# First block's q by seven products, the gate's sums behind the exponentials, one copy per slot handed to VectorE in slots 12 to 15

## The chip, the cores and the metric

The kernel runs on one core of one Trainium2 chip. The metric is the device time of one execution in microseconds (us). The kernel before took 3244.99 us, the median of three executions (3246.35, 3242.94 and 3244.99). TensorE multiplies, VectorE and ScalarE read its results out of PSUM, GpSimd does a few tiny steps, and SyncE only issues DMAs. Every engine works through its own instructions in the order in which they are written.

## The reference

A sequence of 4 x 2048 tokens of width 512 passes through windowed attention and then through a feed-forward layer whose weights are blended per group of tokens. All is float32.

```
x = x + layernorm(attention(layernorm(x)))       # 16 heads of 32, windows of 128 tokens
x = x + layernorm(ffn(layernorm(x)))

attention:  q, k, v = x @ w_qkv
            each window of 128 queries sees its own and both neighbouring windows of keys
            softmax over up to 384 keys, then attn @ v
ffn:        h = relu(x @ gate_w1.T + gate_b1)
            g = mean over tokens of (h @ gate_w2.T + gate_b2)        # 8 numbers per batch
            mW1 = W1 + sum_e g[e] * TW1[e] ;  mW2 = W2 + sum_e g[e] * TW2[e]   # 2048 x 512
            out = gelu(x @ mW1.T + mb1) @ mW2.T + mb2
```

## The kernel before, in words

**Two stages.** The attention stage does windowed attention for all 64 windows, and along with it the gate and the first part of the blending. The feed-forward stage follows it on the same core and blends the rest while it multiplies.

**Blocks, windows, slots.** A block is 512 tokens (16 blocks, `K`), a window 128 tokens (64, `W_`). A window is done in four slots of four heads each, so there are 256 slots; slot `i` belongs to window `i // 4` and group `g = i % 4`. The main loop issues for slot `i`, in this order: the scores of slot `i + 1` (`scores`, L599, and their negated row maxima on VectorE, L608); the transposes of the probabilities of slot `i` for each of its two or three key windows `j` (`turn`: TensorE L636, then a copy from PSUM to `prT`, L638); the lists `mid`; the exponentials of slot `i + 1` on ScalarE (`exponentials`, L621); the dense products of a later block (`dense`); the list `rest`; the blending; the reads of the dense products; and, in every second slot, the products with v (`values`, L654). Scores and exponentials are in float32 in a pair of PSUM tiles (`ps_s`, two tiles), both of which belong to one slot: the next slot's scores cannot be written before the four exponentials have read them.

**Projections by seven products.** A 512-wide projection of a block is done as a two-by-two block product with seven instead of eight half-size products (`products`, `product`, `produced`; in the loop `paired`, `pair_read`). It needs sums and differences of the weights' quarters (`left_factors`, four VectorE operations) and of the token block's quarters (`right_factors`, two operations in each of two parts), and several products are accumulated in one PSUM bank, which is read between them. For block 0 this is done for k and v only; its q is done by sixteen whole matmuls (`project`, L403), ahead of them. Block 0 is projected before the loop starts; there the four tiles of block 1 are normalized and transposed too (`place_tile`).

**The gate.** For blocks 0 to 13 the gate's first layer is done by seven products too, in the four slots `s0` to `s0 + 3`, with `s0 = 4 * (4 * (K + 3) - 5)` (28, 44, 60, 76, ...) for the earlier blocks. Its result stands in four quarters; each is put through ScalarE's relu, with the sum over tokens taken along (`gate_quarter_sum`, two ScalarE operations per quarter, L175). One quarter is summed straight from PSUM at the end of slot `s0 + 3`. The three others are summed from SBUF at the start of slots `s0 + 3`, `s0 + 4` and `s0 + 5`, ahead of the transposes' copies (list `early_reads`). The last block of a batch is followed by `means`, `experts`, `first_biases` and `second_biases` (`gate_end`), in slots `s0 + 5` to `s0 + 7`.

**The blending.** A generator (`mixer`) yields one step at a time: eight multiply-adds on VectorE over 128 x 1024 (L144), each on a 512 KB block that SyncE fetched three steps ahead, then one step of sums, and again. From slot 84 on, the list `MIXED` says how many steps each slot takes, by the slot's number modulo 16 (20 steps in 16 slots). The feed-forward stage takes fixed numbers of steps and stops when there are none left.

Of the kernel before, what the change touches and what calls it, by code (L numbers as in the profile page):

```python
# [9 lines left out]
F32 = mybir.dt.float32  # L10
# [6 lines left out]
P = 128  # L17
# [4 lines left out]
KC = D // P  # L22
TB = 512
WB = TB // W
# [6 lines left out]
QSCALE = float(E) ** -0.5  # L31
# [3 lines left out]
def sandwich(ctx: ExitStack, tc: tile.TileContext, x, w_qkv, gw1, gb1, gw2, gb2, w1, b1, w2, b2, tw1, tb1, tw2, tb2, out):  # L35
    nc = tc.nc
# [14 lines left out]
    Q = D // 2  # L51
# [280 lines left out]
    with ExitStack() as actx:  # L332
# [3 lines left out]
        ps_t = actx.enter_context(tc.tile_pool(name="ps_t", bufs=3, space=PSUM))  # L336
# [32 lines left out]
        def norm_stats(K, t):  # L369
            xs_of[K, t] = stats(x_of[K, t], f"a{K}_{t}")  # L370

        def norm_tile(K, t):
            xn = xn_of[K, t] = x_of.pop((K, t))
            normalize(xn, xn, xs_of.pop((K, t)))
# [13 lines left out]
        def projection(K, i):  # L388
            if i == 0 and K % 2 == 0:
                return wp.tile([P, KC, TB], F32, tag="q0", name=f"q_{K}")  # L390
            return qkvp.tile([P, KC, TB], F32, tag="qkv"[i], bufs=2 if i else 1, name=f"{'qkv'[i]}_{K}")

        def project(K, i, m, pm, kcs=range(KC)):

            if m == 0 and kcs[0] == 0:
                (q_of, k_of, v_of)[i][K] = projection(K, i)
            xnT = xnT_of[K]
            for kc in kcs:
                if i < 2:
                    l, r = wqkv[i][:, kc, ts(m, P)], xnT[:, kc, :]  # L400
                else:
                    l, r = xnT[:, kc, ts(m, P)], wqkv[2][:, kc, :]
                nc.tensor.matmul(pm, lhsT=l, rhs=r, start=(kc == 0), stop=(kc == KC - 1))  # L403

        def projected(K, i, m, pm):
            if i == 0:
                nc.scalar.mul(q_of[K][:, m, :], pm, QSCALE)
            elif i == 1:
                nc.vector.tensor_copy(k_of[K][:, m, :], pm)
            else:  # L410
                nc.scalar.copy(v_of[K][:, m, :], pm)

# [28 lines left out]
        lefts, rights, bank = {}, {}, {}  # L444
# [75 lines left out]
        def product(K, i, u, half, key=0):  # L520
            l, r, begins, _, _ = products[u]
            if begins and half == 0 and key:
                sc = ps_s.tile([P, 2, TB], F32, tag="sc", name=f"pm_{K}_{i}_{u}")
                bank[key] = sc[:, 0, :].rearrange("p (a b) -> p a b", a=2)
            elif begins and half == 0:
                bank[0] = ps_m.tile([P, 2, Q], F32, tag="pm", name=f"pm_{K}_{i}_{u}")
            if u < 2 and half == 0:
                rights.setdefault((K, False), {"11": xnT_of[K][:, :2, :Q], "21": xnT_of[K][:, 2:, :Q]})
            left, right = lefts[i][l], rights[K, False][r]
            for kc in range(2):  # L530
                a, b = (left, right) if i < 2 else (right, left)
                nc.tensor.matmul(  # L532
                    bank[key][:, half, :],
                    lhsT=a[:, kc, ts(half, P)],
                    rhs=b[:, kc, :],
                    start=(begins and half == kc == 0),
                    stop=True,
                    skip_group_check=True,
                )
# [90 lines left out]
        def turn(i, j):  # L630

            W_, g = divmod(i, KC)
            st = win[W_]
            pt = ps_t.tile([P, 4, W], F32, tag="pt", name=f"ptp_{i}_{j}")
            for r in range(4):
                nc.tensor.transpose(pt[:, r, :], st["pr"][g * 4 + r][:, ts(j, W)], ident)  # L636
            prT = work.tile([P, 4, W], F32, tag="prT", bufs=6, name=f"prT_{i}_{j}")
            nc.scalar.copy(prT, pt)  # L638
            st["prT"][g, j] = prT

        def values(i, n):
# [31 lines left out]
        first = {i: [] for i in slots}  # L673
        mid = {i: [] for i in slots}
        late = {i: [] for i in slots}
        early_reads = {i: [] for i in slots}
        for K in range(1, NBK):
            s0 = 4 * (4 * K - 5)
            if K > 1:
# [61 lines left out]
        for K, s0 in gate_at.items():  # L741
            first[s0 - 2].append(lambda K=K: load_gate(K))
            if K < 14:
                for part in range(2):
                    rest[s0 + part].append(lambda K=K, part=part: right_factors(K, part, 3))
                for g in range(KC):
                    dense[s0 + g] = (
                        lambda half, K=K, g=g: [
                            paired(K, 3, u, h)
                            for u in ((others[g], chain[g]) if others[g] is not None and half == 0 else (chain[g],))  # L750
                            for h in ((0, 1) if u not in chain else (half,))
                        ],
                        lambda K=K, g=g: gate_read(K, g, 0),
                        lambda K=K, g=g: gate_read(K, g, 1),
                    )

                for j, (row, col) in ((3, (0, 1)), (4, (1, 1)), (5, (0, 0))):
                    early_reads[s0 + j].append(
                        lambda K=K, row=row, col=col: gate_quarter_sum(K, row, col, quarter[row, col], quarter[row, col])
                    )  # L760
                if K % NBLK == NBLK - 1:
                    b = K // NBLK
                    means, experts, first_biases, second_biases = gate_end(b, hsum_of[b], spare_bank, spare)
                    rest[s0 + KC + 1].append(means)

                    mid[s0 + KC + 2].append(experts)
                    mid[s0 + KC + 3].append(second_biases)
                    rest[s0 + KC + 3].append(first_biases)
                continue
            for oc in range(KC):  # L770
                dense[s0 + oc] = (
                    lambda half, K=K, oc=oc: gate_tile(K, oc, half),
                    lambda K=K, oc=oc: gate_sum(bank[0], K, oc, hsum_of[K // NBLK], spare),
                )
# [102 lines left out]
        for t in range(WB):  # L877
            x_of[1, t] = load_tile(1, t, "x", 4)
        load_rest()

        sums = [
            lambda: left_factors(1),
            lambda: right_factors(0, 0),
            lambda: left_factors(2),
            lambda: right_factors(0, 1),
        ]
        for m in range(KC):
            pm = ps_t.tile([P, KC, P], F32, tag="pt", name=f"pm0_{m}").rearrange("p k t -> p (k t)")
            project(0, 0, m, pm)
            projected(0, 0, m, pm)  # L890
            sums[m]()
        for u in range(7):
            for i in (1, 2):
                for half in range(2):
                    product(0, i, u, half, i)
                produced(0, i, u, i)
            if u < WB:
                norm_stats(1, u)
            if 1 <= u <= WB:
                norm_tile(1, u - 1)  # L900
            if 2 <= u <= WB + 1:
                place_tile(1, u - 2, nc.vector.tensor_copy)
            if u == 2:
                left_factors(0)
        scores(0)
        exponentials(0, range(4))


        MIXED = (1, 0, 1, 1, 2, 1, 1, 2, 2, 1, 1, 1, 2, 1, 1, 2)
        for i in range(NS):  # L910
            W_, g = divmod(i, KC)
            nk = span_of(W_)[1]
            for f in first[i]:
                f()
            if i + 1 < NS:
                scores(i + 1)
            more = i + 1 < NS
            for f in early_reads[i]:
                f()
            for j in range(nk):  # L920
                turn(i, j)
            for f in mid[i]:
                f()
            if more:
                exponentials(i + 1, range(4))
            for f in aux[i]:
                f()
            if dense[i]:
                dense[i][0](0)
                dense[i][0](1)  # L930
            for f in rest[i]:
                f()
            if dense[i] and len(dense[i]) > 2:
                dense[i][2]()
            if i >= 84:
                for _ in range(MIXED[i % 16]):
                    next(blend)
            if dense[i]:
                dense[i][1]()
            if i >= PAIRS:  # L940
                for n in (i - 1, i) if i == PAIRS else (i,):
                    values(n, 0)
            elif i % 2 == 0:
                if i:
                    values(i - 1, 0)
                values(i, 1)
            for f in late[i]:
                f()
# [407 lines left out]
```

## Time and profile before

| what | value |
|---|---|
| median of three executions | 3244.99 us |
| profiled execution, its time / its span | 3242.52 us / 3240.1 us |
| TensorE busy | 3217.5 us (99% of the span) |
| TensorE weight loads busy | 2686.7 us (83%), beside the matmuls |
| VectorE busy | 2146.4 us (66%) |
| ScalarE busy | 1565.3 us (48%) |
| GpSimd busy | 665.9 us (21%) |
| mean granted TensorE clock | 0.999 |

"Busy" is the time in which an instruction of the engine was running. A busy TensorE can still be stretched: its matmuls' ends are modelled, so a matmul that waits shows in the distance between two starts before it shows as idle time. In a timeline row the columns are the start in us from the span's start, the length, the engine, the line, the operation, what it writes and reads, the shape, how many instructions were merged into the row, and, in brackets, the engine's idle time before it and what ended it. A float32 matmul shows as two instructions.

### The profile page before, as it was taken

Reading aid. Unit: us, or ns where it says so; the run is one execution under the profiler, and the core shown is the slowest. Engines: PE = TensorE matmul, PEld = TensorE weight load, DVE = VectorE, ACT = ScalarE, POOL = GpSimd, SP = SyncE. Lnnn points to the kernel's source line nnn. Section 1 sums busy time; section 2 is a strip of 40 time slices with the busy share of each in tenths; the row PEclk is TensorE's granted clock in tenths of the full one; section 3 lists DMA queues with packets and bytes.
Section 4 is the critical chain, followed back from the end, with each engine's and each line's share of the span. In section 5 each row is a group of like instructions: output and inputs, shape, how many; then the busy total and the mean of one; then the engine's idle time right before and its main releaser. Section 6 shows DMA issues by size and latency. Waiting matters only on the chain.

```text
span 3240.1 us, 59233 instructions
## 1 busy us (share of the span) xinstructions
PE 3217.5 (99%) x23166; PEld 2686.7 (83%) x23166; DVE 2146.4 (66%) x2989; ACT 1565.3 (48%) x4291; POOL 665.9 (21%) x843
## 2 busy tenths in 40 slices
PE   9999999999999999999999999999999999999999
PEld 7787878888787887878768888888888888888888
DVE  5666666888888888888865665667657776412212
ACT  3767777777777777777761222112222111222121
POOL 1111111111111111110012332323332323321222
PEclk9999999999999999999999999999999999999999
DMA  2111112455555445554577889998889998822332
GB/s 86 50 53 58 42 53 79 145 165 171 191 180 177 155 160 199 189 175 148 200 264 276 317 311 347 351 335 327 317 323 361 340 335 328 305 104 91 130 111 98
DMA packets 316120, 652.00 MB, mean 201 GB/s; under 512 B 22969, under 2 KB 89657, under 8 KB 295490
## 3 DMA queue, kind: packets, MB, share of 16 engines
q1 hardware_dynamic: 315842, 648.22, 57.2%
q8 instruction: 183, 3.00, 0.4%
q14 instruction: 95, 0.78, 0.1%
HBM read 538.03 MB, written 110.10 MB: 200 GB/s over the span
## 4 chain that ended last, share of the span: by engine, by line
PE 94%; DVE 2%; ACT 2%; DMA 1%; issue 0%; POOL 0%; SPq 0%; POOLq 0%; ACTq 0%; DVEq 0%
PE pm L473 22%; PE px L971 13%; PE ptp L636 10%; PE px L1069 10%; PE pz L1069 7%; PE pz L971 7%; PE sc L599 6%; PE po L654 5%; PE py L971 3%; PE py L1069 3%; PE py2b L1069 3%; DMA exps<-in_tw 1%; PE ptx L287 1%; PE pto L258 1%; PE pt_a L382 1%; PE pm L532 1%
## 5 line engine op out<-in xcount | busy, mean ns | idle before, releaser
L144 DVE SCALAR_TENSOR_TENSOR acc<-exps,g,acc 128x1024 f32<-128x1024 f32 x512 | 703.6, 1374 | 77.9 <-DMA exps<-in_tw 72.5
L608 DVE TENSOR_REDUCE nm<-sc 128x2 f32<-128x768 f32 (+1 forms) x512 | 449.9, 919 | 229.6 <-PE sc L599 224.4
L621 ACT ACTIVATE pr<-sc,nm 128x384 f32<-128x384 f32 (+1 forms) x1024 | 574.0, 595 | 9.1 <-DVE nm L608 8.9
L638 ACT COPY prT<-ptp 128x512 f32<-128x512 f32 x736 | 384.8, 595 | 262.1 <-PE ptp L636 261.2
L1008 ACT COPY py<-px 128x512 f32<-128x512 f32 x63 | 36.0, 571 | 783.8 <-PE px L971 783.6
L636 PEld LDWEIGHTS ptp<-ident,pr 128*128 128x128 f32 x2944 | 317.2, 141 | 102.0 <-issue 89.6
L636 PE MATMUL ptp<-ident,pr 128*128 128x128 f32 x2944 | 378.0, 278 | 0.0
L971 PE MATMUL px<-tT,w 128*128 128x256 f32 x1512 | 349.7, 379 | 0.6 <-DVE cpv L1031 0.6
L971 PEld LDWEIGHTS px<-tT,w 128*128 128x128 f32 x1512 | 287.1, 190 | 40.2 <-DVE cpv L1031 1.2
L599 PE MATMUL sc<-k,q 32*128 32x384 f32 (+2 forms) x2816 | 243.6, 422 | 5.7 <-ACT pr L621 5.5
L621 ACT ACTIVATION_READ_ACCUMULATOR pr<-sc,nm 128x1 f32 x1024 | 238.2, 233 | 0.0
L1069 PE MATMUL px<-w2s,u 128*128 128x256 f32 x1024 | 228.9, 379 | 0.7 <-ACT last L292 0.7
L1028 DVE TENSOR_TENSOR cpb<-pz,cpb 128x512 f32<-128x512 f32 x63 | 43.5, 690 | 280.0 <-PE pz L971 245.9
L1069 PEld LDWEIGHTS px<-w2s,u 128*128 128x128 f32 x1024 | 194.5, 190 | 27.3 <-ACT last L292 0.9
L91 POOL TENSOR_SCALAR ve_b<-mv_b 128x1 f32<-128x1 f32 x64 | 42.0, 657 | 819.2 <-DVE mv_b L89 819.2
L654 PEld LDWEIGHTS po<-prT,v 128*32 128x32 f32 x5888 | 152.2, 110 | 50.8 <-ACT pr L621 26.8
L654 PE MATMUL po<-prT,v 128*32 128x128 f32 x5888 | 189.7, 275 | 0.1
L599 PEld LDWEIGHTS sc<-k,q 32*128 32x128 f32 x2816 | 119.3, 183 | 76.8 <-issue 54.3
L1046 POOL TENSOR_TENSOR t<-u 128x512 f32<-128x512 f32 x64 | 84.9, 1326 | 463.2 <-ACT u L983 451.1
L473 PE MATMUL pm<-xnT,wqkv 128*128 128x256 f32 x720 | 173.4, 384 | 0.0
L1088 DVE TENSOR_TENSOR y<-px,mb 128x512 f32<-128x512 f32 x48 | 33.1, 690 | 192.8 <-PE px L1069 192.8
L473 PEld LDWEIGHTS pm<-xnT,wqkv 128*128 128x128 f32 x720 | 133.0, 191 | 19.1 <-ACT prT L638 2.3
(230 smaller groups left out, 5601.8 us busy)
## 6 DMA issues: line engine op xcount, KB each, us to landing
exps<-in_tw SPq DMA_DIRECT2D x512, 512.0 KB, 6.3
w2s<-m2d SPq DMA_DIRECT2D x112, 1024.0 KB, 7.2
acc<-in_w SPq DMA_DIRECT2D x64, 512.0 KB, 6.6
x<-in_x SPq DMA_DIRECT2D x64, 256.0 KB, 4.5
m1d<-acc SPq DMA_DIRECT2D x64, 256.0 KB, 6.7
m2d<-acc SPq DMA_DIRECT2D x64, 256.0 KB, 6.5
w<-m1d SPq DMA_DIRECT2D x16, 1024.0 KB, 7.8
fxT<-xTd SPq DMA_DIRECT2D x16, 1024.0 KB, 8.9
```

What stands on the lines that cost most here:

```text
L144: nc.vector.scalar_tensor_tensor(acc, ets.pop(n), g_all[b][:, e : e + 1], acc, ALU.mult, ALU.add)
L473: nc.tensor.matmul(bank[u not in chain][:, half, :], lhsT=a[:, kc, ts(half, P)], rhs=b[:, kc, :], start=(u not in (2, 3, 4) and half == kc ...
L599: nc.tensor.matmul(scs[r // 2][:, r % 2, col : col + nj * W], lhsT=q[rows, g, ts(W_ % WB, W)], rhs=k_of[kb][rows, g, j0 * W : (j0 + nj) * ...
L608: nc.vector.tensor_reduce(st["nm"][:, h : h + 2], scs[u][:, :, : nk * W], AX.X, ALU.max, negate=True)
L621: nc.scalar.activation(pr[:, : nk * W], scs[r // 2][:, r % 2, : nk * W], AF.Exp, bias=st["nm"][:, h : h + 1], accum_out=st["den"][:, h : h ...
L636: nc.tensor.transpose(pt[:, r, :], st["pr"][g * 4 + r][:, ts(j, W)], ident)
L638: nc.scalar.copy(prT, pt)
L654: nc.tensor.matmul(po[r * E : (r + 1) * E, n, :], lhsT=v_of[kb][:, jj, h * E : (h + 1) * E], rhs=prT[:, r, :], start=(j == 0), stop=(j == ...
L971: nc.tensor.matmul(bank[:, f, :], lhsT=factor[:, f, kc * P : (kc + 1) * P], rhs=right[:, kc, :], start=(start and f == 0 and kc == 0), sto ...
L1028: nc.vector.tensor_tensor(S["b"], Z, S["b"], ALU.add)
L1046: nc.gpsimd.tensor_tensor(t1s[c], b12, us[c][:, :, :Q], ALU.subtract)
L1069: nc.tensor.matmul(bank[:, t, :], lhsT=right(c - c % 2)[:, c % 2, ts(t, P)], rhs=w[:, c, :], start=(start and c == 0 and t == tiles[0]), s ...
```

## The change

Four things are changed.

1. The first block's q is done by the seven products as well. The three projections of block 0 now alternate: q, k, v of product 0, then of product 1, and so on. q and k use the two `ps_s` tiles for their banks, v uses the `ps_m` bank. The factors' sums come in another order (`right_factors(0, 0)` and `left_factors(0)` first), and block 1's tiles are normalized and placed at other points; the last two of them are copied out by ScalarE instead of VectorE. v's products 5 and 6 stand behind the first scores and exponentials.
2. The three quarter sums of the gate are issued at the end of slots `s0 + 2`, `s0 + 5` and `s0 + 6`, behind that slot's exponentials and dense reads, instead of at the start of `s0 + 3`, `s0 + 4` and `s0 + 5`. What follows at a batch's end (`means` to `second_biases`) is issued two slots later.
3. In slots 12 to 15 the copy of the third key window's transposes is done by VectorE instead of ScalarE.
4. The blending starts in slot 85 instead of 84, and slots with number 14 modulo 16 take two steps instead of one.

```diff
@@ product
-            left, right = lefts[i][l], rights[K, False][r]
+            if i in lefts:
+                left = lefts[i][l]
+            else:
+                j = int(l) - 11
+                left = wqkv[i][:, 2 * j : 2 * j + 2, :Q]
+            right = rights[K, False][r]
@@ turn
-            nc.scalar.copy(prT, pt)
+            if j == 2 and 12 <= i < 16:
+                nc.vector.tensor_copy(prT, pt)
+            else:
+                nc.scalar.copy(prT, pt)
@@ gate
-                for j, (row, col) in ((3, (0, 1)), (4, (1, 1)), (5, (0, 0))):
-                    early_reads[s0 + j].append(
+                for j, (row, col) in ((2, (0, 1)), (5, (1, 1)), (6, (0, 0))):
+                    behind[s0 + j].append(
                         lambda K=K, row=row, col=col: gate_quarter_sum(K, row, col, quarter[row, col], quarter[row, col])
                     )
-                    rest[s0 + KC + 1].append(means)
-                    mid[s0 + KC + 2].append(experts)
-                    mid[s0 + KC + 3].append(second_biases)
-                    rest[s0 + KC + 3].append(first_biases)
+                    rest[s0 + KC + 3].append(means)
+                    mid[s0 + KC + 4].append(experts)
+                    mid[s0 + KC + 5].append(second_biases)
+                    rest[s0 + KC + 5].append(first_biases)
@@ ahead of the loop
-        sums = [left_factors(1), right_factors(0, 0), left_factors(2), right_factors(0, 1)]   # as lambdas
-        for m in range(KC):
-            pm = ps_t.tile([P, KC, P], F32, tag="pt", name=f"pm0_{m}").rearrange("p k t -> p (k t)")
-            project(0, 0, m, pm)
-            projected(0, 0, m, pm)
-            sums[m]()
-        for u in range(7):
-            for i in (1, 2):
-                for half in range(2):
-                    product(0, i, u, half, i)
-                produced(0, i, u, i)
-            if u < WB:
-                norm_stats(1, u)
-            if 1 <= u <= WB:
-                norm_tile(1, u - 1)
-            if 2 <= u <= WB + 1:
-                place_tile(1, u - 2, nc.vector.tensor_copy)
-            if u == 2:
-                left_factors(0)
-        scores(0)
-        exponentials(0, range(4))
-        MIXED = (1, 0, 1, 1, 2, 1, 1, 2, 2, 1, 1, 1, 2, 1, 1, 2)
+        right_factors(0, 0)
+        left_factors(0)
+        between = {
+            (0, 2): [lambda: left_factors(1)],
+            (1, 1): [lambda: left_factors(2)],
+            (1, 2): [lambda: right_factors(0, 1)],
+            (2, 2): [lambda: norm_stats(1, 0), lambda: norm_stats(1, 1)],
+            (3, 1): [lambda: norm_tile(1, 0), lambda: norm_tile(1, 1)],
+            (3, 2): [lambda: norm_stats(1, 2), lambda: norm_stats(1, 3)],
+            (4, 1): [lambda: norm_tile(1, 2), lambda: norm_tile(1, 3)],
+            (4, 2): [lambda: place_tile(1, 0, nc.vector.tensor_copy)],
+            (5, 1): [lambda: place_tile(1, 1, nc.vector.tensor_copy)],
+            (6, 1): [lambda: scores(0), lambda: exponentials(0, range(4))],
+            (5, 2): [lambda: place_tile(1, 2, nc.scalar.copy)],
+            (6, 2): [lambda: place_tile(1, 3, nc.scalar.copy)],
+        }
+        turns_of = [(u, i) for u in range(5) for i in range(3)] + [(5, 0), (5, 1), (6, 0), (6, 1), (5, 2), (6, 2)]
+        for u, i in turns_of:
+            key = (1, 2, 0)[i]
+            for half in range(2):
+                product(0, i, u, half, key)
+            produced(0, i, u, key)
+            for f in between.get((u, i), ()):
+                f()
+        MIXED = (1, 0, 1, 1, 2, 1, 1, 2, 2, 1, 1, 1, 2, 1, 2, 2)
@@ loop over slots
-            for f in early_reads[i]:
-                f()
             for j in range(nk):
                 turn(i, j)
...
-            if i >= 84:
+            if i >= 85:
                 for _ in range(MIXED[i % 16]):
                     next(blend)
             if dense[i]:
                 dense[i][1]()
+            for f in behind[i]:
+                f()
```

`left_factors`, `right_factors`, `norm_stats`, `norm_tile`, `place_tile`, `scores` and `exponentials` are the same functions as before.

More of the change, by code (lines that the diff above doesn't have):

```diff
@@ L391, in projection @@
             return qkvp.tile([P, KC, TB], F32, tag="qkv"[i], bufs=2 if i else 1, name=f"{'qkv'[i]}_{K}")
[L393 to L411, printed above, removed]
         def left_factors(i):
@@ L675, in sandwich @@
         late = {i: [] for i in slots}
-        early_reads = {i: [] for i in slots}
+        behind = {i: [] for i in slots}
         for K in range(1, NBK):
@@ L879, in sandwich @@
         load_rest()
[L881 to L886, printed above, removed]
-        for m in range(KC):
-            pm = ps_t.tile([P, KC, P], F32, tag="pt", name=f"pm0_{m}").rearrange("p k t -> p (k t)")
-            project(0, 0, m, pm)
-            projected(0, 0, m, pm)
-            sums[m]()
-        for u in range(7):
-            for i in (1, 2):
-                for half in range(2):
-                    product(0, i, u, half, i)
-                produced(0, i, u, i)
-            if u < WB:
-                norm_stats(1, u)
-            if 1 <= u <= WB:
-                norm_tile(1, u - 1)
-            if 2 <= u <= WB + 1:
-                place_tile(1, u - 2, nc.vector.tensor_copy)
-            if u == 2:
-                left_factors(0)
-        scores(0)
-        exponentials(0, range(4))
-        MIXED = (1, 0, 1, 1, 2, 1, 1, 2, 2, 1, 1, 1, 2, 1, 1, 2)
+        right_factors(0, 0)
[23 more added lines that the diff above has]
+        MIXED = (1, 0, 1, 1, 2, 1, 1, 2, 2, 1, 1, 1, 2, 1, 2, 2)
         for i in range(NS):
```

## The prediction

> **What bounds the kernel now.** I read the page first: TensorE is busy for 3217.5 of 3240.1 us, so a change pays only through less matmul work or where TensorE stands still or runs slowly. TensorE's waits come next.
>
> ```profile
> PE 3217.5 (99%) x23166; PEld 2686.7 (83%) x23166; DVE 2146.4 (66%) x2989; ACT 1565.3 (48%) x4291; POOL 665.9 (21%) x843
> ```
>
> ```profile
> PE sc L599 <- ACT pr L621: 5.5, 11, 1.5
> PE ptx L287 <- ACT prT L638: 2.8, 10, 0.3
> PE pm L473 <- ACT prT L638: 1.8, 3, 0.6
> ```
>
> The columns are total, times, longest. All three name ScalarE as releaser. TensorE's timeline says where they lie: from the first block into slot 1, then in slots 13 to 16.
>
> ```profile
> 12.18 14.00 PE L403 MATMUL pm<-xnT,wqkv 128*128 128x512 f32 x32 [0.23 <-ACT xnT L384]
> 26.02 1.89 PE L532 MATMUL pm<-xnT,wqkv 128*128 128x256 f32 x8
> 27.75 1.89 PE L532 MATMUL pm<-wqkv,xnT 128*128 128x256 f32 x8
> ...
> 52.45 0.70 PE L599 MATMUL sc<-k,q 32*128 32x256 f32 x4
> 53.30 0.70 PE L599 MATMUL sc<-k,q 32*128 32x256 f32 x4 [0.15 <-DVE v L552]
> 55.00 0.70 PE L599 MATMUL sc<-k,q 32*128 32x256 f32 x4 [0.99 <-ACT pr L621]
> 55.91 0.70 PE L599 MATMUL sc<-k,q 32*128 32x256 f32 x4 [0.21 <-ACT pr L621]
> 56.54 1.51 PE L636 MATMUL ptp<-ident,pr 128*128 128x128 f32 x8
> 57.85 3.19 PE L473 MATMUL pm<-xnT,wqkv 128*128 128x256 f32 x8
> ...
> 62.19 1.09 PE L636 MATMUL ptp<-ident,pr 128*128 128x128 f32 x8
> ...
> 140.20 1.53 PE L636 MATMUL ptp<-ident,pr 128*128 128x128 f32 x12
> 141.57 0.63 PE L382 MATMUL pt_a<-ident,x 128*128 128x128 f32 x4
> ...
> 149.08 0.93 PE L599 MATMUL sc<-k,q 32*128 32x128 f32 x8 [1.46 <-ACT pr L621]
> ```
>
> Start to start, a product of four matmuls takes 1.73 us (26.02 to 27.75); the one at 57.85 took 3.13. The view by stretches says why: the granted clock was halved there. Its columns are length, the five engines' busy times with counts, clock, DMA.
>
> ```profile
> 57.06:60.48 3.42, 3.42 (x13) 2.86 (x12) 1.58 (x3) 2.97 (x10) 0.00 (x0) 0.50 0.00 0
> ```
>
> The gate's cost shows on ScalarE, here in slot 80:
>
> ```profile
> 560.86 1.53 PE L636 MATMUL ptp<-ident,pr 128*128 128x128 f32 x12
> 561.05 0.50 ACT L175 ACTIVATE g<-g,gb_sb 128x256 f32<-128x256 f32 x1
> 562.04 1.55 ACT L638 COPY prT<-ptp 128x512 f32<-128x512 f32 x3
> 562.67 0.66 PE L287 MATMUL ptx<-ident,x 128*128 128x128 f32 x4 [0.28 <-ACT prT L638]
> ```
>
> The copies normally start 0.70 us after the transposes (140.20, copy at 140.90), which would be 561.56; the early sum holds them until 562.04. TensorE then needs a buffer that the first copy frees: twelve transposes to the next group take 1.81 us, against 1.37 (140.20 to 141.57).
>
> **Part 1, the head.** Removed: sixteen whole matmuls, 13.84 us (12.18 to 26.02). Added: seven products, 7 x 1.73 = 12.11. That alone is 1.7 us less matmul work. For the rest I follow TensorE through the new order.
>
> The start stays at 12.18. The three weights landed at 10.15, 12.86 and 15.57 (the issue rows' landings) and are wanted at 12.18, 13.91 and 15.64: v's leaves 0.07, which I take as no wait. VectorE does six factor operations at 0.68 from 12.2 and four more, until 19.0; the first sums are wanted at 22.56 (six products later). left_factors(2) runs from 21.6 to 24.3, wanted at 26.0. Each bank is read while the two other projections multiply, 3.46 us, against reads of 0.6 to 0.7. So no wait until product 6: the 15 products of rounds 0 to 4 end at 38.13, a tile (0.43) and q's and k's product 5, another tile and their product 6 end at 45.9.
>
> The first half of scores(0) starts at 45.9; the second waits for VectorE's read of k's product 6, until 46.76, and ends at 47.4 (now the same: 53.30 after 52.45). v's product 5 runs to 49.13, a tile to 49.56, then 0.4 us of waiting for VectorE's read of that bank (0.69 plus latency), v's product 6 to 51.71, a tile to 52.14. scores(1) starts at 52.14, against 55.00. The exponentials of slot 0 are over by 49.4, so their release, 0.99 + 0.21 us now, is covered by v's two products. If these were shorter, the release at 49.4 would still precede 52.14 by 2.7 us.
>
> Next: transposes at 52.78, a product at full clock 53.7 to 55.4, values to 56.0. ScalarE copies a tile of block 1 until 52.85, the transposes until 54.5, then four exponentials at a pitch of 0.455 until 56.45. The second half of scores(2) waits for these, so slot 1's transposes start at 57.2, against 62.19: **5.0 us gained**, 2.9 up to scores(1) and 2.1 behind it, of which the half clock is 3.42 x 0.5 = 1.7. I take the clock at full because TensorE was busy for 2.21 of the 3.41 us ahead of the half-clock stretch, partly with scores of 0.70 each, and in the new order no 3.4 us stretch has under 2.5 us, mostly full products. Ends: 1.7 (matmul work alone, ScalarE setting the rest) and 6.2 (none of the three waits, 0.2 + 0.4 + 0.6).
>
> The Trainium skill, "TensorE: Matmul & The Clock Gate", Part 1, says that the gate halves the clock after an idle window of about 3.4 us and that the windows run freely. Its window length agrees with the 3.42 us here. By it the halving depends on where the window falls, so it need not have struck the other executions of the kernel before; then 1.7 us of my gain would not be there.
>
> **Part 2, slots 12 to 15.** They hold no dense products, and ScalarE's round sets them: fourth exponential over, second half of scores (0.86), transposes (0.70 to the first copy), three copies (0.52 pitch), four exponentials (2.24 in all). The round is 5.43 us (138.22 to 143.65 to 149.08). With two copies on ScalarE it is 0.5 shorter per slot, as long as the row maxima are there: in slot 14 the second ended at 141.3 and the exponentials began at 142.33, one copy earlier is 141.8. VectorE's copy, 0.69 us (the row of block 1's tiles), runs behind the maxima and is wanted only by values, about 1 us later; VectorE was busy for 4.55 of 5.43 us there, less in the other three. Slot 12 gains 0.5 on ScalarE, hidden by TensorE. Slot 13's xnT, xo and oT copies then finish at 134.7 instead of 135.2 and three copies become two, so its exponentials start 1.2 earlier and slot 14's scores follow 1.4 earlier; slots 14 and 15 add 0.6 each. Sum: **2.6 us**. Ends: 0 (maxima set the round instead) and 6.7, all that slots 13 to 16 exceed the time of the same matmuls elsewhere.
>
> **Part 3, the gate's sums.** Each costs ScalarE 1.0 us (two at a 0.5 pitch). Ten blocks lose 1.81 - 1.37 = 0.44, with the slot 6.46 long; three at a batch's start lose 0.9 (slot 65: 464.60 to 466.73 is 2.13 against 1.37, and its scores 0.17 more). 4.5 + 2.7 is 7.2; the block of slot 240 may give 0.3: **7.5 us**. In their new places they must fit ahead of the next copies. End of s0 + 2: ScalarE was free from 551.69 to 553.75, waiting for values. End of s0 + 5: free from 572.33 to 574.38, 2.0 us less the 0.5 at most by which slots move. End of s0 + 6: 2 us of waiting for values again. All are over 1.0. If that cover is gone, the copies behind are late by the excess, as now. The other end is 0: every wait comes back one slot on.
>
> At a batch's end, means to second_biases move two slots on, each over two slots that have transposes of their own. Same instructions, means still four us behind the sums; the DMA of the bias moves with them on SP, behind one more xo store. Between 0 and 0.5 x 3; I take 0, as slots 81 to 83 show no TensorE wait.
>
> **Part 4, the blending.** Eleven slots gain a multiply-add of 1.28 us, slot 84 loses two: nine more, exactly one round of eight and a sum, so the feed-forward stage does its work in the same phase, nine steps earlier. In slot 94 VectorE has the room:
>
> ```profile
> 658.43 0.68 DVE L730 TENSOR_TENSOR g<-pm,g 128x512 f32<-128x512 f32 x1
> 660.61 1.82 DVE L608 TENSOR_REDUCE nm<-sc 128x2 f32<-128x768 f32 x2 [1.49 <-PE sc L599]
> ```
>
> 1.28 fits in the 1.49 that it waits ahead of slot 95's maxima. SP issues one more 512 KB load in these slots; no multiply-add of the attention stage waits for one (the 72.5 us of such waits all lie in the feed-forward stage). Taken at 0, ends -1.9 (three feed-forward waits of 0.8, 0.7 and 0.6 gone, roughly) and +2.
>
> **Sum.** 5.0 + 2.6 + 7.5 = 15.1 us. The profiled execution took 3242.52 (2.4 outside its span) and would take 3227.4; the median is 2.5 higher, so 3244.99 - 15.1 = **3229.9 us**, 0.47% less.
>
> **The rivals.**
> - *The half clock was this execution's.* Gain 13.4, 3231.6. For it: the halving began on one particular stretch; against it: that stretch's stall is in the program's order.
> - *ScalarE sets the new head.* It has two tile copies more. Gain 1.7 + 2.6 + 7.5 = 11.8, 3233.2. Against it: it idles from 49.4 to 52.25 but for one copy.
> - *The moved sums wait again*, at s0 + 6 behind the sum of s0 + 5, where the margin is 0.5 to 1.0 us. Gain 7.6, 3237.4. That is also the case of a move that does nothing.
> - *Slower: the extra multiply-add waits for its block.* VectorE stands before L144 in eleven slots, and the maxima, exponentials and scores behind it stand too. A load lands 6.3 us after issue in the median, 11.7 at worst, and SP stood 340.8 us behind xo stores in this stage. It decides from 2.0 us per slot ((15.1 + 6.5) / 11); at 3 us it is 33 - 15 = 18 slower, 3263. Against it: the load goes out three steps ahead, and at today's 20 steps in 16 slots no wait occurs.
>
> **Chances and range.** Likeliest 0.60 (its own range 3226 to 3233), half clock 0.08, ScalarE 0.10, sums 0.10, slower 0.05, several small losses to between 3238 and 3250 0.07. This kernel's measurement can tell 0.2%, 6.5 us: faster is below 3238.5. The first four, less a part of the sums case, give 0.86; same 0.08; slower 0.06. The range is 3224 (the upper ends of parts 1 and 2 partly reached, 21 us) to 3239.
>
> **What would show it.** No half clock after 57; slot 1's transposes near 57; TensorE's wait for pr down from 5.5 to under 4; both rows that wait for prT gone; a round of 4.9 in slots 14 and 15; VectorE's wait of 1.49 down to 0.2. I would be wrong if L144 waits for its DMA before slot 255, or if prT waits reappear at s0 + 6.

## The result, and the profile after

The changed kernel took 3231.59 us, the median of six executions (3227.71 to 3233.09), against 3244.85 us for the kernel before on the same chip. The ratio is 0.996, with a 95% interval from 0.995 to 0.9971: 13.3 us faster, where 15.1 were forecast. The profiled execution took 3230.53 us, 12.0 less than the profiled one of before, so the sum below is made for 12.0.

The head of the page of the kernel after:

```profile
span 3228.7 us, 59302 instructions
...
PE 3211.8 (99%) x23190; PEld 2690.1 (83%) x23190; DVE 2142.8 (66%) x2995; ACT 1566.3 (49%) x4288; POOL 660.1 (20%) x843
```

TensorE is busy for 5.7 us less. Its waits in the kernel after (total, times, longest):

```profile
PE sc L584 <- ACT pr L606: 3.3, 9, 1.0
PE pt_a L382 <- DVE x L98: 1.4, 3, 0.7
PE idle L855 <- POOL ident masks.py:199: 1.3, 1, 1.3
PE pm L517 <- DMA wqkv<-in_w_qkv: 1.0, 2, 0.8
```

Both rows that waited for `prT` are gone, and the wait for `pr` is down from 5.5 to 3.3. The fourth row is new: TensorE waits for a weight. The timeline of the kernel after shows where, and what the other parts became:

```profile
11.29 1.89 PE L517 MATMUL pm<-xnT,wqkv 128*128 128x256 f32 x8
13.36 1.99 PE L517 MATMUL pm<-xnT,wqkv 128*128 128x256 f32 x8 [0.18 <-DMA wqkv<-in_w_qkv]
16.16 1.97 PE L517 MATMUL pm<-wqkv,xnT 128*128 128x256 f32 x8 [0.80 <-DMA wqkv<-in_w_qkv]
17.96 3.62 PE L517 MATMUL pm<-xnT,wqkv 128*128 128x256 f32 x16
...
46.55 0.70 PE L584 MATMUL sc<-k,q 32*128 32x256 f32 x4
47.41 0.70 PE L584 MATMUL sc<-k,q 32*128 32x256 f32 x4 [0.15 <-DVE k L537]
48.04 1.99 PE L517 MATMUL pm<-wsum,tx_False 128*128 128x256 f32 x8
...
50.82 1.99 PE L517 MATMUL pm<-wsum,xnT 128*128 128x256 f32 x8 [0.35 <-DVE v L537]
...
53.18 0.71 PE L584 MATMUL sc<-k,q 32*128 32x256 f32 x8
...
58.11 1.09 PE L621 MATMUL ptp<-ident,pr 128*128 128x128 f32 x8
...
135.14 1.53 PE L621 MATMUL ptp<-ident,pr 128*128 128x128 f32 x12
...
140.08 1.53 PE L621 MATMUL ptp<-ident,pr 128*128 128x128 f32 x12
...
554.54 1.53 PE L621 MATMUL ptp<-ident,pr 128*128 128x128 f32 x12
555.23 1.56 ACT L626 COPY prT<-ptp 128x512 f32<-128x512 f32 x3 [0.39 <-PE ptp L621]
555.90 0.62 PE L287 MATMUL ptx<-ident,x 128*128 128x128 f32 x4
```

Without waits the three products would start 1.73 us apart, at 11.29, 13.02 and 14.75; the third starts at 16.16, 1.41 late. Slot 1's transposes stand at 58.11 instead of 62.19. A round of slots 13 to 15 is 4.94 us (135.14 to 140.08) instead of 5.43. In slot 80 (the last three rows) the copies now start 0.69 behind the transposes, and the next group follows after 1.36, not 1.81.

And the half clock is still there, in the view by stretches (length, busy times of the five engines, clock, DMA):

```profile
57.06:60.48 3.42, 3.42 (x31) 2.82 (x24) 2.49 (x4) 2.68 (x9) 0.00 (x0) 1.00 0.00 0
144.62:148.04 3.42, 3.42 (x19) 2.77 (x16) 2.90 (x5) 1.17 (x2) 0.00 (x0) 0.50 0.01 2
141.20:144.62 3.42, 2.26 (x22) 1.58 (x22) 2.63 (x6) 3.38 (x11) 1.00 (x2) 1.00 0.04 13
```

It left the head, and struck slots 15 and 16 (the third row is the window ahead of it). The start of each slot's transposes, compared between the two profiled executions, gives the account:

| place | forecast, us | measured, us |
|---|---|---|
| first product, 12.18 to 11.30 | 0 | 0.89 |
| head, first product to slot 1 | 5.0 | 3.20 |
| slots 12 to 15 | 2.6 | 1.62 |
| half clock in slot 16 | 0 | -1.27 |
| gate's sums, slots 17 to 240 | 7.5 | 7.59 |
| slot 247 | 0 | -1.02 |
| feed-forward stage | 0 | 0.42 |
| outside the span (2.38 to 1.82) | 0 | 0.56 |
| sum | 15.1 | 12.0 |

The loss in slot 247 has this row on VectorE, which the kernel before does not have:

```profile
1620.67 0.55 DVE L98 TENSOR_SCALAR x<-x,mv_c,rs_c 128x512 f32<-128x512 f32 x1 [3.35 <-DMA x1d<-x]
```

The normalization overwrites `x1` in place, and waits until `x1` is stored.

### The profile page after: what moved, and what is told of

The parts are those of the page before. It is cut to its first block, busy times and chain, and to the rows that moved or that the text cites. A ratio compares the mean times of both kernels' runs of the same rounds, so it can differ in the third digit from the quotient of the medians.

```text
span 3228.7 us, 59302 instructions
## 1 busy us (share of the span) xinstructions
PE 3211.8 (99%) x23190; PEld 2690.1 (83%) x23190; DVE 2142.8 (66%) x2995; ACT 1566.3 (49%) x4288; POOL 660.1 (20%) x843
## 4 chain that ended last, share of the span: by engine, by line
PE 96%; DMA 2%; DVE 1%; ACT 1%; issue 0%; POOL 0%; SPq 0%; POOLq 0%; DVEq 0%; ACTq 0%
PE pm L453 23%; PE px L958 13%; PE ptp L621 11%; PE px L1056 10%; PE sc L584 7%; PE pz L958 7%; PE pz L1056 6%; PE po L642 5%; PE py L958 3%; PE py L1056 3%; PE py2b L1056 3%; DMA exps<-in_tw 1%; PE pm L517 1%; PE ptx L287 1%; PE pto L258 1%; PE pt_a L382 1%
## 5 line engine op out<-in xcount | busy, mean ns | idle before, releaser
L144 DVE SCALAR_TENSOR_TENSOR acc<-exps,g,acc 128x1024 f32<-128x1024 f32 x512 | 697.0, 1361 | 75.0 <-DMA exps<-in_tw 69.0
```

Of the source, the lines that this page charges most:

```text
L144: nc.vector.scalar_tensor_tensor(acc, ets.pop(n), g_all[b][:, e : e + 1], acc, ALU.mult, ALU.add)
```

## The experiments

**First, the parts apart.** Four kernels ran on one chip, where the kernel before took 3244.1 us. The first is the kernel before with the gate's sums moved, and nothing else:

```diff
-                for j, (row, col) in ((3, (0, 1)), (4, (1, 1)), (5, (0, 0))):
-                    early_reads[s0 + j].append(
+                for j, (row, col) in ((2, (0, 1)), (5, (1, 1)), (6, (0, 0))):
+                    behind[s0 + j].append(
...
-                    rest[s0 + KC + 1].append(means)
+                    rest[s0 + KC + 3].append(means)
```

> The kernel before with the gate's sums moved and nothing else. If the sums' place is what held the transposes' copies: ten slots shorten by 0.47 us each and three by 0.96 (the steps that the changed kernel shows at slots 32, 48, 65, 80 and so on), 7.6 us in all, and TensorE waits for no prT copy any more; about 3237 us. If part of that gain came from the slots' new position in time (the head's 4 us earlier, other DMA neighbours), fewer than 7 us. The half clock at 57 us stays.

It took 3235.96 us, ratio 0.9976 (0.9966 to 0.9985): 8.1 us. In its trace ten slots are 0.47 shorter and three pairs of slots at a batch's start 0.96, 7.6 in all, in the same slots as in the kernel after. The gate's part stands alone, at its forecast. The half clock at 57, which was expected to stay, is not in this profile; three others are.

The second is the kernel after with the gate's sums, the copies and the blending of before, so only the head is new:

```diff
-            if j == 2 and 12 <= i < 16:
-                nc.vector.tensor_copy(prT, pt)
-            else:
-                nc.scalar.copy(prT, pt)
+            nc.scalar.copy(prT, pt)
...
-                for j, (row, col) in ((2, (0, 1)), (5, (1, 1)), (6, (0, 0))):
-                    behind[s0 + j].append(
+                for j, (row, col) in ((3, (0, 1)), (4, (1, 1)), (5, (0, 0))):
+                    early_reads[s0 + j].append(
...
-            if i >= 85:
+            if i >= 84:
```

> The kernel before with the first block's new order and nothing else. Theory: slot 1's transposes come 3 to 4.1 us earlier than before (3.2 counted from the first product), v's weights are waited for again (0.8 to 1.1 us behind the second product), and no half clock follows at 57 us. Now the stretch in slots 12 to 16 is the kernel before's (rounds of 5.43 us): if low activity there is what halves the clock, it should be halved in slots 15 to 17 here too, or not at all if the windows fall otherwise; if it was the copy on VectorE that brought the half clock to 145 us, it stays at full.

It took 3238.17 us, ratio 0.9982 (0.9973 to 0.9992): 5.9 us. In its profile slot 1 starts 4.93 earlier, of which 1.3 is an earlier first product (10.86). Here a half clock began at 146.68 and took 1.65 back, and the feed-forward stage took 1.1 more than in the profile of before.

The third is the kernel before with VectorE's copy in slots 12 to 15:

```diff
-            nc.scalar.copy(prT, pt)
+            if j == 2 and 12 <= i < 16:
+                nc.vector.tensor_copy(prT, pt)
+            else:
+                nc.scalar.copy(prT, pt)
```

> The kernel before with the third copy of slots 12 to 15 on VectorE and nothing else. Theory: 0.49 us earlier per slot from slot 13 on, 1.6 to 2.1 us by slot 16's transposes. If the half clock depends on where its window falls, the head's half clock at 57 us is kept and slots 16 and 17 may run at full clock, 2 us gained at slot 17; if the copy itself brings it (TensorE less busy in each window of slots 14 to 16), it is halved at 145 to 151 us too and 0.3 us is left.

Its one execution took 3244.6 us, so the time tells nothing; its trace does. Slots 12 to 15 are 0.49 shorter each, 1.96 in all. Nothing is hidden in slot 12 and nothing is doubled in slot 13: every round is shorter by about one copy at ScalarE's pitch. And its clock was halved in four windows, in three places. Each row with a clock of 0.50 below is preceded by the window ahead of it:

```profile
51.59:55.00 3.41, 2.27 (x14) 0.90 (x12) 2.02 (x3) 1.76 (x8) 0.00 (x0) 1.00 0.00 0
55.00:61.83 6.83, 6.62 (x26) 4.77 (x28) 2.67 (x4) 3.21 (x13) 0.00 (x0) 0.50 0.01 2
147.16:150.58 3.42, 2.51 (x23) 1.78 (x24) 2.80 (x6) 2.29 (x10) 1.00 (x2) 1.00 0.03 5
150.58:153.99 3.41, 3.41 (x16) 3.14 (x15) 2.12 (x4) 3.05 (x8) 0.00 (x0) 0.50 0.00 0
1601.24:1604.65 3.41, 2.45 (x37) 1.31 (x38) 3.30 (x6) 3.20 (x11) 0.29 (x2) 1.00 0.87 317
1604.65:1608.06 3.41, 3.41 (x19) 2.76 (x16) 2.79 (x4) 0.98 (x2) 0.50 (x1) 0.50 0.62 187
```

Ahead of each halving TensorE was busy for 2.3 to 2.5 of 3.41 us.

The fourth is the kernel after with the old blending:

```diff
-            if i >= 85:
+            if i >= 84:
...
-        MIXED = (1, 0, 1, 1, 2, 1, 1, 2, 2, 1, 1, 1, 2, 1, 2, 2)
+        MIXED = (1, 0, 1, 1, 2, 1, 1, 2, 2, 1, 1, 1, 2, 1, 1, 2)
```

> The changed kernel with the old blending (from slot 84, one step in slots of number 14 modulo 16). If the nine steps that were brought forward are what puts the store of window 61's x1 among other transfers, the wait of VectorE for that store in slot 247 (3.35 us, which cost 1.0 us of TensorE) is gone; the feed-forward stage then is as long as before, 0.4 us more than in the changed kernel: 0.6 us less in sum. If that wait is chance or comes from the earlier arrival, it stays. Everything up to slot 240 within 0.1 us of the changed kernel, but for the clock's windows.

It took 3229.51 us, ratio 0.9955 (0.9938 to 0.9971). The wait in slot 247 is gone. By chance its first product, at 10.86, found v's weights landed at 14.19 and its products stand 1.73 apart: the head is the one that I forecast, 45.42 us from the first product to slot 1's transposes. It lost 1.09 to a half clock in slot 242, and its feed-forward stage took 1.4 more than in the profile of before, where the same length was expected.

**What the half clock follows.** Each of the six profiles so far shows it, in changing places. If a window with little matmul work is the cause, idle matmuls put into the thin slots must remove it from all. The next kernel is the fourth with such matmuls, whose result nothing reads; the computation is complete:

```diff
+        FILL = {13: 3, 14: 3, 15: 4, 240: 2, 241: 4}
...
+            if i in FILL:
+                filler = ps_m.tile([P, P], F32, tag="pm", name=f"fill_{i}")
+                for _ in range(FILL[i]):
+                    nc.tensor.matmul(filler, lhsT=ident, rhs=ident, start=True, stop=True)
```

> The changed kernel with the old blending, and with 3, 3, 4, 2 and 4 idle matmuls of 0.21 us behind slots 13, 14, 15, 240 and 241, where TensorE waits for exponentials. Theory: the clock is halved for 3.41 us after a window of 3.41 us in which the array did less than about 1.2 to 1.4 us of full-array work; with 0.6 to 0.9 us more in each window none stays under 1.5, so no half clock stands between 10 and 3200 us. It costs up to 0.3 us where the idle matmuls outlast the wait, and gains 1.0 to 1.7 us per half-clock stretch avoided, 2 us on average over executions: a median of 3227 to 3229 and a smaller spread. Rival: the halving goes by standing still, not by the array's work, or by something else; then half-clock stretches stand in these slots as before and the time is the same or 0.5 us worse.

It took 3228.87 us, ratio 0.9954 (0.9941 to 0.9966), and no stretch between the first products and the end is at half clock. Its median is no proof of a gain: the intervals of this ratio and the fourth's overlap. In this execution TensorE waited 0.8 us for v's weights again.

The next one also puts v's first product one place later, behind q's and k's:

```diff
-        turns_of = [(u, i) for u in range(5) for i in range(3)] + [(5, 0), (5, 1), (6, 0), (6, 1), (5, 2), (6, 2)]
+        turns_of = [(0, 0), (0, 1), (1, 0), (0, 2), (1, 1), (1, 2)] + [(u, i) for u in range(2, 5) for i in range(3)] + [(5, 0), (5, 1), (6, 0), (6, 1), (5, 2), (6, 2)]
```

> The same, and in the first block v's product 0 stands behind q's product 1, so that v's weights are wanted 1.73 us later. Theory: the weights land between 14.2 and 16.0 us, by execution, and v's product 0 wanted them 3.5 us after the first product: now 5.2 us after it, at 16 or later, so no wait for v's weights (k's may wait 0.2 to 0.3), and slot 1's transposes come 45.4 to 45.8 us after the first product in every execution; 0 to 1.1 us gained by execution, 0.5 in the median. Rival: VectorE's factors or the reads of the banks become late by the new order; then waits for VectorE appear at the first block's products.

It took 3227.36 us, ratio 0.9951 (0.9938 to 0.9963). Its timeline has no wait for weights; 24 matmuls run through:

```profile
11.42 5.35 PE L517 MATMUL pm<-xnT,wqkv 128*128 128x256 f32 x24
16.61 1.89 PE L517 MATMUL pm<-wqkv,xnT 128*128 128x256 f32 x8
```

The later versions with this order never wait for v's weights either, but two of their three profiles wait 0.38 and 0.25 for k's. Their heads take 45.99 and 45.85 us from the first product to slot 1's transposes, against 45.34 without any wait.

The same idle matmuls in the kernel before, with four more behind its first exponentials (both kernels already have some ahead of their first products; "with idle matmuls" means those added here):

```diff
         exponentials(0, range(4))
+        keep_busy(4)
...
+        FILL = {13: 3, 14: 3, 15: 4, 240: 2, 241: 4}
```

> The kernel before with the same idle matmuls and four more behind the first exponentials. Theory: half-clock stretches are gone from the head too, where three executions of the old order showed none, one and two of them (0, 1.4 and 2.8 us): about 1.4 us in the median there and 2 in the later slots, 3240 to 3242 us against 3244, and less spread. That would be the part of the changed kernel's gain that needed no other order of the work. Rival: no difference, if the halving doesn't go by the array's work.

It took 3240.72 us against 3242.67, ratio 0.9993 (0.9984 to 1.0003). No stretch is at half clock here either. Its head takes 48.66 us from the first product to slot 1's transposes, against 50.01 in the profile of before: the half clock there cost 1.35 us.

The stretches of half clock in all thirteen profiles, between the first products and the last ones:

| kernel | starts, us (3.41 us each) |
|---|---|
| before | 57.06 |
| after | 144.62 |
| gate only | 138.69, 148.93, 1596.18 |
| head only | 146.68 |
| copy only | 55.00 (two windows), 150.58, 1604.65 |
| after, old blending | 1589.42 |
| blending only | 149.13 |
| the six with idle matmuls | none |

Is it the time in which TensorE is busy, or the work that it does? Two windows at the same place, each with the window behind it, answer it: the first pair is from the kernel before, the second from the kernel before with the new blending alone (the next experiment), which is the same program up to slot 84.

```profile
145.81:149.22 3.41, 1.95 (x18) 1.68 (x19) 2.14 (x4) 2.89 (x8) 1.00 (x2) 1.00 0.00 0
149.22:152.63 3.41, 3.22 (x30) 2.44 (x31) 2.40 (x3) 2.28 (x7) 0.00 (x0) 1.00 0.02 5
145.72:149.13 3.41, 1.96 (x18) 1.23 (x19) 1.16 (x3) 2.80 (x10) 0.80 (x2) 1.00 0.02 5
149.13:152.54 3.41, 3.41 (x17) 3.41 (x17) 2.66 (x4) 2.02 (x4) 0.00 (x0) 0.50 0.00 0
```

TensorE was busy for 1.95 and 1.96 us of the first and the third row, and only the window behind the third was halved. Busy time alone does not decide it. What differs is which matmuls stood there. In the first window they are nearly all transposes, which use the array's 128 rows and 128 columns; in the third most are scores, which use 32 of the rows (`128*128` and `32*128` in the timeline rows). Counted as under "What is open" below, an estimate, the first held 1.6 us of whole-array work and the third 0.9.

**The blending.** The kernel before with the new blending alone ran beside the last three:

```diff
-            if i >= 84:
+            if i >= 85:
...
-        MIXED = (1, 0, 1, 1, 2, 1, 1, 2, 2, 1, 1, 1, 2, 1, 1, 2)
+        MIXED = (1, 0, 1, 1, 2, 1, 1, 2, 2, 1, 1, 1, 2, 1, 2, 2)
```

> The kernel before with the new blending alone. Theory: the nine steps brought forward cost nothing up to slot 240 and 1.0 us in slot 247 (VectorE waits over 3 us for the store of x1), give 0.4 us in the feed-forward stage: 0 to 1.5 us slower than before, not to be told from it. If slot 247 shows no wait, that wait was chance in the changed kernel's execution. If slots of number 15 modulo 16 lose time, VectorE has no room for the second step.

It took 3244.8 us, ratio 1.0007 (0.9998 to 1.0016). Its slot 247 waits too, for 5.2 us, and ends 2.9 us late, with nothing gained in the feed-forward stage (-0.07). To find the mechanism three more ran together, with idle matmuls so that no half clock blurs them. One is the version with v later, with the new blending:

> The version with idle matmuls and v's second product later, but with the blending of the kernel after (from slot 85, two steps in the slots with number 14 modulo 16). Theory (the phase of the round): in slots 239 to 253 the new blending is eight steps ahead, not nine, so the group of the blended matrix's stores and the reload of the next blocks is issued around slots 244 and 245 instead of 241, and the 256 KB store of x1 (slot 245) lands behind it some 7 us after its issue instead of 3.4; the normalization that overwrites x1 waits 3 to 5 us for it on VectorE and slot 247 ends 1.0 to 2.9 us late. No half-clock stretch. 1 to 3 us slower than the same kernel with the old blending in this call. Rival (the blending costs nothing, and the two slot-247 waits seen were single executions): same time within 0.7 us, no such wait.

It took 3229.87 us (3228.41 to 3230.57), ratio 0.9957 (0.9942 to 0.9971), with this on SyncE and VectorE:

```profile
1601.89 0.49 SPq L125 DMA_DIRECT2D m1d<-acc  x1
1602.48 0.40 SPq L126 DMA_DIRECT2D m1d<-sums  x1
1602.98 0.43 SPq L127 DMA_DIRECT2D m1d<-sums  x1
1603.46 1.16 SPq L128 DMA_DIRECT2D m1d<-acc  x1
1604.72 1.16 SPq L319 DMA_DIRECT2D w<-m1d  x2
...
1610.79 0.34 SPq L278 DMA_DIRECT2D x1d<-x  x1
...
1618.88 0.55 DVE L98 TENSOR_SCALAR x<-x,mv_c,rs_c 128x512 f32<-128x512 f32 x1 [4.27 <-DMA x1d<-x]
```

The next takes one step more in slot 237 and one less in slot 254:

```diff
-                for _ in range(MIXED[i % 16]):
+                for _ in range(MIXED[i % 16] + (i == 237) - (i == 254)):
```

> As the run before, with one more step of blending in slot 237 and one less in slot 254, so that slots 238 to 253 are nine steps ahead, a whole round. Theory (the phase): the group is issued around slot 241 again, the store of x1 lands within 3.5 us, no wait for it in slot 247; the time is that of the old blending within 0.7 us, or up to 0.5 us less. Rival (any blending that is ahead loads more in slot 245 and holds the store up): the wait in slot 247 stays at 3 to 5 us, and 1 to 3 us are lost as in the run before.

It took 3227.44 us (3226.49 to 3227.8), ratio 0.9949 (0.9936 to 0.9962). The four stores are issued 12 us earlier, and the wait is gone:

```profile
1589.56 0.49 SPq L125 DMA_DIRECT2D m1d<-acc  x1
1590.10 0.43 SPq L126 DMA_DIRECT2D m1d<-sums  x1
1590.57 0.48 SPq L127 DMA_DIRECT2D m1d<-sums  x1
1591.10 1.43 SPq L128 DMA_DIRECT2D m1d<-acc  x1
...
1602.09 0.94 SPq L319 DMA_DIRECT2D w<-m1d  x2
...
1610.95 0.34 SPq L278 DMA_DIRECT2D x1d<-x  x1
...
1614.69 0.54 DVE L98 TENSOR_SCALAR x<-x,mv_c,rs_c 128x512 f32<-128x512 f32 x1
```

The last is the version with v later and the old blending again.

> The version with idle matmuls, v's second product later and the old blending once more, as the partner of the two runs before on the same chip. Both theories: 3226 to 3229 us if the kernel before takes 3243, no wait for the store of x1 in slot 247, no half-clock stretch in the main loop.

It took 3227.1 us (3226.78 to 3227.47), ratio 0.9948 (0.9935 to 0.9961). The executions of the new blending lie wholly above those of the two others: the phase of the round, and not the earlier start, costs 2.4 to 2.8 us. This last version and the one with the shifted steps are the best; the last has a ratio of 0.9948 to the kernel before where the kernel after has 0.996. The two were not run side by side, and their intervals overlap a little.

## Why the prediction was right, and where it was not

**The whole.** The forecast of 3229.9 us was 1.7 us under the median of 3231.59, for 15.1 forecast against 13.3. The terms erred more than the sum, so the nearness is luck in part: in the profiled execution 1.8 was missed in the head, 1.0 in slots 12 to 15, 1.3 in slot 16 and 1.0 in slot 247, and 1.9 came from three places where nothing was forecast. The median is also the 3231.6 of the rival "the half clock was this execution's", but with these other misses in it, so the number does not single that rival out.

**The gate's sums (7.5 forecast, 7.6 measured).** This is the term that carried the result, and the reading behind it held: copies late behind a sum, one PSUM buffer late behind the copies. The 0.44 per block was 0.47 (ten times 0.44 is 4.4; the sum had 4.5), the 0.9 at a batch's start 0.96. The 0.3 of slot 240 did not come. Moving the batch's end by two slots cost nothing, as taken.

**The head (5.0 forecast, 3.2 measured).** Two steps failed. The first is v's margin of 0.07 us, "which I take as no wait". It was counted from weights and a first product of the same execution, but both move: v's weights landed at 16.02 in the kernel after, and at 14.19, 14.34, 15.18 and 15.19 in the profiles of the first four experiments. In the kernel after the weights were 0.4 to 0.5 later than in the profile of before and the first product 0.89 earlier, and 1.41 us were lost. The fourth experiment, without the wait, has the 45.42 us that I worked out as 45.02; v's first product one place later has 45.34 in its profile. Against the old order at full clock (48.66, the kernel before with idle matmuls) that is 3.2 less, where the forecast without the half clock was 3.3: the reading of the order itself held.

The second is the half clock. "Of which the half clock is 1.7" was 1.35, and the step from "no 3.4 us stretch has under 2.5 us" in the new head to a full clock was right for the head but not for the execution: slots 14 to 17 and 241 to 243 are thin as well, in both kernels. So the gain at 57 was paid back at 144.62. The rival "the half clock was this execution's" had the mechanism: the kernel before, with its head untouched, shows none there in two of the profiles (gate only, blending only) and two windows in another. The Trainium skill, "TensorE: Matmul & The Clock Gate", Part 1, has windows of 3413 ns that run freely; the stretches of 3.41 us, whose places change from execution to execution, agree with it, and what I drew from it (that the halving need not strike every execution at 57 us) came true. Its condition of an idle window does not agree: TensorE was busy for 1.8 to 2.5 of 3.4 us in the window ahead of every such stretch, and the measurement decides. That the windows run freely shows within an execution too: each stretch starts a whole number of windows of 3.413 us after the moment from which the trace records full clock (5.86 us in the kernel before and 15 windows, 51.20 us, to 57.06; 4.68 in the kernel after and 41 windows, 139.94 us, to 144.62).

**Slots 12 to 15 (2.6 forecast, 1.6 measured, 1.96 without the half clock).** The round of 4.9 came out as 4.94. The step that failed is the one on slots 12 and 13, where I had 0.5 hidden and then 1.4; the 0.6 each of slots 14 and 15 was too much as well. Each of the four slots gains 0.49. VectorE's copy cost nothing, as expected.

**The blending (0 forecast; 1.0 lost in slot 247 of the profiled execution, 2.4 to 2.8 at the median of the runs made for it).** The step "in the same phase, nine steps earlier" failed. Nine more is right only from slot 254 on; in slots 239 to 253 it is eight, and a round is nine. So the four stores of the blended matrix and the reload behind them fell just ahead of the store of `x1`. The rival of a slower kernel had the right kind of mishap, a transfer late behind blending traffic with VectorE standing before it, but the wrong transfer: L144 never waited before the feed-forward stage, and VectorE's 1.49 in slot 95 went to 0.17, as forecast (0.2).

**What offset these.** The first product stood 0.89 earlier, and 0.56 less lay outside the span. Both vary between executions of the same kernel: its first product stood at 12.18 in the profile of before, and at 11.3 to 11.5 in the four experiments with the old head. The 0.42 of the feed-forward stage is no gain that is shown: from the transposes of slot 255 to the end the thirteen profiles take 1561.2 to 1563.0 us, with the old blending and the new.

**What is open.** What a window must hold to keep the clock. An estimate that counts every matmul of the traces by its columns (1.69 ns each, from sixteen matmuls of 512 in 13.84 us at full clock) and by its share of the 128 by 128 array (the scores use 32 rows, the products with v 32 columns) gives 0.6 to 1.4 us of whole-array work in all windows before a halving. Windows of 1.2 to 1.4 went both ways, and above that none was halved. Idle matmuls removed the halving in six of six profiles, where seven of seven without them had it. In five of the six the thinnest window held 1.7 us or more; in the kernel before with idle matmuls one held 1.3 and kept its clock, in the range that went both ways. What the idle matmuls gain at the median was not separated from the rest (about 2 us in the kernel before, with an interval that includes none).

## What to carry to other kernels

Take a transfer's margin from several executions: 0.07 us between a landing and its use was a wait in three of the four profiles with that order, and giving the late operand one more place in the order cost nothing. When periodic background work is shifted, count its phase at each place where something else needs the queue, not only at the end. And a stall that is taken away need not give back the slow clock behind it, if other thin stretches remain for the next window to fall on.

## What the runs showed of the hardware

The granted clock halved behind windows in which TensorE was far from idle, for exactly one window (3.41 us) or two, in seven of the seven profiles without idle matmuls, while the mean clock still read 0.997 to 0.999. Sixteen small idle matmuls at the ends of five thin slots kept it at full speed in the kernel after, and with four more behind the first exponentials in the kernel before.

A store of 256 KB that follows blended-matrix stores, reloads and two loads of 512 KB on SyncE's queue took some 7 us until VectorE could go on (in the kernel after from its issue at 1613.50 to 1620.67), and 8.1 in the run with the new blending and v later. With the reload issued 9 instead of 6 us ahead, and the four stores 12 us earlier, it was through within 3.7 us (1610.95 to 1614.69). The traces show what landed just ahead of it: the 512 KB load issued before it landed 0.8 us before VectorE went on, in all three profiles with the wait (in the kernel after at 1619.90, 10.6 us after its issue, where in the kernel before that load took 6.5). The Trainium skill, "DMA: Bandwidth & Descriptors", "Queues, rings and completion order", says that the signal of a DMA's end lands only after every earlier write of the same DMA engine; the delay agrees with that, though no run here takes one cause of it from another.
